# A written order for the first turns of a 64-unit pipeline, with two units begun beside the second Gram matrix

## The chip, the cores and the metric

The kernel runs on one core of one Trainium2 chip, as one launch, with all data in float32. The metric is device time in microseconds (us). The kernel before took 2868.09 us as the median of three runs (2866.86 to 2873.42).

## What is computed

The input is `x` of shape (16, 32, 128, 128). Two residual layers follow each other.

```
# layer 0
n = group_norm(x, 16 groups)
q, k, v = projections of n: 8 images are stacked into 256 channels, 8 heads of 64
x = x + Wout . (softmax(q k^T / 8) v) + bout        # attention over channels, not pixels
# layer 1
w = group_norm(x), in windows of 8x8 pixels;  y = layernorm(w) over the 32 channels
a = kan(y, groups of 16 along the window's height)  # kan(t): exp(-((layernorm(t) - g_i) / d)^2) for 8 g_i,
d = kan(y, groups of 16 along its width)            #   times a matrix, + silu(t) times a matrix, + bias
e = kan(y, the 32 channels)
out = x + w + kan(a + d + e, the 32 channels)
```

## The kernel before

**Layer 0 as a matrix.** Attention runs over channels, so all that it needs from the pixels is a 256 x 256 Gram matrix for each group `bp` of eight images. Two groups make two Gram matrices. `gram_load` brings 16 blocks of 2 MB (SP issues one half of a block, ACT the other), `gram_turn` transposes them on DVE (64 turns `m`, four to a block, into two alternating buffers, so turn m waits until turn m-2 has been summed), and `gram_sum` multiplies on PE (four strips of eight matmul records to a turn). `attention(bp)` then makes a matrix `pts[bp]` in 49 short steps that alternate between PE, DVE and ACT. Step 0 and 1 of `attention(1)` read the second Gram matrix out of its PSUM buffer and free it.

**Layer 1 as 64 units.** A unit is 128 partitions by 1024 values. Units 0 to 31 belong to the first eight images and need `pts[0]`; units 32 to 63 need `pts[1]`. For each unit, tasks run one after another:

- `load` (one transfer for two units), `layer0_norm` (PE steps 0, 2, 5; ACT steps 1, 3, 4, 6), `keep` (spills the unit to DRAM), `rows_norm` (PE step 0; DVE steps 1 to 3), `move` (eight transfers that exchange rows and partitions, `d<-yy`).
- `norm_a` and `norm_b` (PE steps 0, 4, 6; ACT steps 1, 2, 3, 5), `scale_a` and `scale_b` (DVE, two steps, line 1140), `seed_a` and `seed_b` (ACT, four steps of exponentials), `ladder_a` and `ladder_b` (DVE, seven products of basis functions, line 1169), `silus` (ACT).
- `products_a` and `products_b` (PE, accumulating in both PSUM buffers named X), `evict_a`, `move_back` (`ad_r<-ad`), `evict_z`; the sum of a unit goes through `norm_b` and `products_b` once more two turns later; then `again`, `result`, `store`.

In what follows, `norm_a.0.1` is step 0 of `norm_a` for unit 1, and `attention.21.1` is step 21 of `attention(1)`; the lists in the code count in the same way (name, step, unit or units behind).

**The order.** All engines execute their instructions in the order in which they are issued, and the kernel fixes that order itself. `Flow.run` holds all tasks as generators, keeps a planned time for each engine and each buffer, and repeatedly issues one step. `ORDER` gives, for PE, ACT, DVE and SP, the steps of one turn, with how many units behind each step is; `Flow.orders` repeats it for all turns. In `run`, the first step of an engine's list that isn't done and whose unit is below `first` is that engine's due step; steps that no list names (Gram matrices, attention, parameters) are fitted in where they are ready before the due step. `first` is `AHEAD` until the second Gram matrix is planned, and all units after that:

```
first = AHEAD if UNTIL not in self.found else units
```

With `AHEAD` 1, only unit 0 is taken up while the second Gram matrix is being summed.

**Buffers that matter here.** PSUM has two buffers X and two buffers Y. A Gram matrix holds one X; a unit's products take both X, so no product is issued before the second Gram matrix is finished and copied. `norm` takes both Y for its step 0 and for its step 6. There are six tiles `u`, three `R` and two `yy`; the Gram stage holds two `u`, two `R` and one `yy` until it ends, and the projections hold one `u` and `ad_r` on behalf of attention.

Of the kernel before, what the change touches and what calls it, by code (L numbers as in the profile page):

```python
# [72 lines left out]
    ),  # L73
}

FIRST = {"attention", "projections", "parameters"}
AHEAD, UNTIL = 1, ("gram", 1)
TURNS = 7


# [6 lines left out]
class Flow:  # L87
# [47 lines left out]

    def orders(self, units):

        out = {}
        for engine, text in ORDER.items():
            names = [(name, int(k), int(behind)) for name, k, behind in (t.split(".") for t in text.split())]  # L140
            out[engine] = [(name, m - behind, k) for m in range(units + TURNS) for name, k, behind in names]
        return out

    def run(self, tasks, units):
# [29 lines left out]
        for x in lines:  # L174
            on(x, None)
        heads = dict.fromkeys(orders, 0)
        while True:
            moved = True
# [45 lines left out]
            for c in able:  # L224
                name, engine = c[1]["at"][0], c[1]["asks"][0]
                at, unit = due.get(engine, (c[0] + 1, 0))
                late = c[0] > at or (c[0] == at and unit < AHEAD and name not in FIRST)
                if name in named or late or any(t + PATIENCE <= c[0] and kind in c[1]["asks"][2] for t, kind in kept):
# [1260 lines left out]
```

## Time and profile before

| | before |
|---|---|
| median of 3 runs (range) | 2868.09 us (2866.86 to 2873.42) |
| the profiled execution | 2870.64 us, span 2868.9 us |
| mean granted TensorE clock | 0.985 of full speed |
| busy PE, DVE, ACT (share of the span) | 2746.1 us (96%), 2685.3 us (94%), 2517.7 us (88%) |
| last matmul of the second Gram matrix ends | 221.8 us |
| first matmul of `products_a` | 244.7 us |
| `layer0_norm.0.n` starts, n = 0 to 6 | 145.6, 221.8, 237.8, 276.7, 330.6, 369.2, 409.0 us |

The busy shares are of the whole span; PE's records overlap, since sixteen small matmuls run side by side, so its busy time says that something was in flight, not that the array was full. From `layer0_norm.0.5` on, a turn takes about 39.6 us. Everything that the change touches lies ahead of that.

### The profile page before, as it was taken

Reading aid. Unit: us, or ns where it says so; the run is one execution under the profiler, and the core shown is the slowest. Engines: PE = TensorE matmul, PEld = TensorE weight load, DVE = VectorE, ACT = ScalarE, POOL = GpSimd, SP = SyncE. Lnnn points to the kernel's source line nnn. Section 1 sums busy time; section 2 is a strip of 40 time slices with the busy share of each in tenths; the row PEclk is TensorE's granted clock in tenths of the full one; section 3 lists DMA queues with packets and bytes.
Section 4 is the critical chain, followed back from the end, with each engine's and each line's share of the span. In section 5 each row is a group of like instructions: output and inputs, shape, how many; then the busy total and the mean of one; then the engine's idle time right before and its main releaser. Section 6 shows DMA issues by size and latency. Waiting matters only on the chain.

```text
span 2868.9 us, 100690 instructions
## 1 busy us (share of the span) xinstructions
PE 2746.1 (96%) x45955; PEld 1091.5 (38%) x45955; DVE 2685.3 (94%) x1793; ACT 2517.7 (88%) x2035; POOL 53.8 (2%) x109
## 2 busy tenths in 40 slices
PE   6999999999999999999999999999999999999985
PEld 6874433333333333333333333333333333333321
DVE  4747999999999999999999999999999999999986
ACT  0026899999999999999999999999999999999973
POOL 4200000000000000000000000000000000000000
PEclk9999999999999999999999999999999999999987
DMA  9652233333333333333333333333333333333311
GB/s 243 179 123 60 75 113 110 105 104 113 113 103 98 108 109 116 116 101 110 103 116 113 94 111 100 116 114 108 108 106 111 114 97 103 108 109 114 102 56 35
DMA packets 206152, 311.04 MB, mean 108 GB/s; under 512 B 24480, under 2 KB 156064, under 8 KB 205728
## 3 DMA queue, kind: packets, MB, share of 16 engines
q1 hardware_dynamic: 192512, 285.29, 33.8%
q10 hardware_dynamic: 9504, 16.85, 2.4%
q8 instruction: 362, 5.93, 0.9%
q0 software_dynamic: 3712, 2.46, 0.4%
q14 instruction: 62, 0.51, 0.1%
HBM read 103.18 MB, written 67.11 MB: 59 GB/s over the span
## 4 chain that ended last, share of the span: by engine, by line
PE 64%; DVE 20%; issue 6%; ACT 4%; DMA 4%; SPq 1%; DVEq 0%; ACTq 0%
PE X L436 25%; DVE u L1169 14%; PE X L1205 10%; PE Y L1004 7%; PE Y L436 4%; PE Y L1019 4%; PE X L1324 4%; PE X L684 3%; DVE yc L1140 3%; PE Y L1123 2%; PE Y L981 2%; DVE yy L1057 2%; DMA u<-in_x 1%; SPq L1241 1%; ACT u L1118 1%
## 5 line engine op out<-in xcount | busy, mean ns | idle before, releaser
L1169 DVE SCALAR_TENSOR_TENSOR u<-R,u 128x2048 f32<-128x2048 f32 x910 | 2043.4, 2286 | 38.0 <-ACT u L1154 17.0
L436 PE MATMUL X<-u,wt_a 32*32 32x512 f32 x16384 | 663.8, 605 | 11.2 <-ACT u L1154 4.1
L436 PE MATMUL X<-u,wt_b 32*32 32x512 f32 x16896 | 638.3, 605 | 16.3 <-ACT u L1154 9.4
L436 PEld LDWEIGHTS X<-u,wt_a 32*32 32x32 f32 x16384 | 302.7, 103 | 289.1 <-issue 136.4
L436 PEld LDWEIGHTS X<-u,wt_b 32*32 32x32 f32 x16896 | 224.7, 103 | 384.3 <-issue 194.2
L1140 DVE TENSOR_TENSOR yc<-yc,Y 128x1024 f32<-128x1024 f32 x260 | 305.4, 1216 | 10.6 <-PE Y L1123 7.5
L1149 ACT ACTIVATE u<-yc,vec 128x2048 f32<-128x2048 f32 x130 | 258.5, 1989 | 29.6 <-DVE yc L1140 24.7
L1115 ACT ACTIVATE yc<-Y 128x1024 f32<-128x1024 f32 x260 | 250.2, 1015 | 35.5 <-DMA u<-in_x 22.9
L1004 PE MATMUL Y<-x,pt 128*128 128x512 f32 x512 | 236.7, 605 | 31.5 <-DVE yc L1140 31.5
L1157 ACT ACTIVATE R<-yc,vec 128x2048 f32<-128x2048 f32 x130 | 259.5, 1996 | 2.5 <-DVE u L1169 1.5
L1151 ACT ACTIVATE R<-yc,vec 128x2048 f32<-128x2048 f32 x130 | 258.8, 1991 | 0.0
L1118 ACT ACTIVATE u<-yc 128x2048 f32<-128x2048 f32 x130 | 247.6, 1905 | 2.9 <-DVE u L1169 2.2
L1154 ACT ACTIVATE u<-u 128x2048 f32<-128x2048 f32 x130 | 247.1, 1901 | 0.0
L684 PE MATMUL X<-R 128*64 128x257 f32 (+3 forms) x2048 | 154.4, 312 | 22.8 <-DVE R L658 22.1
L983 ACT ACTIVATE lr<-Y,vec 128x512 f32<-128x512 f32 (+1 forms) x194 | 131.3, 677 | 45.0 <-PE Y L981 45.0
L1004 PEld LDWEIGHTS Y<-x,pt 128*128 128x128 f32 x512 | 92.2, 190 | 179.9 <-issue 92.9
L684 PEld LDWEIGHTS X<-R 128*64 128x64 f32 x2048 | 143.4, 142 | 42.3 <-DVE R L658 23.8
L981 PE MATMUL Y<-u,e 128*32 128x512 f32 x1040 | 139.6, 604 | 3.3 <-ACT u L1118 3.3
L1233 ACT ACTIVATE ad<-X,col 128x1024 f32<-128x1024 f32 x128 | 134.0, 1095 | 1.7 <-PE X L436 1.7
L1019 PE MATMUL Y<-xh,c 128*128 128x512 f32 x256 | 127.0, 618 | 2.4 <-ACT xh L1014 2.4
L984 ACT ACTIVATE lr<-lr 128x512 f32<-128x512 f32 (+1 forms) x194 | 122.4, 631 | 6.2
L1205 PE MATMUL X<-sd,silu_a 64*64 64x512 f32 x1024 | 124.7, 602 | 0.0
(210 smaller groups left out, 2472.9 us busy)
## 6 DMA issues: line engine op xcount, KB each, us to landing
xh<-xh SPq DMA_DIRECT2D x128, 512.0 KB
d<-yy SPq DMA_DIRECT2D x512, 128.0 KB
ad_r<-ad SPq DMA_DIRECT2D x512, 128.0 KB
x<-in_x SPq DMA_DIRECT2D x32, 1024.0 KB
out<-xh SPq DMA_DIRECT2D x256, 128.0 KB
u<-in_x SPq DMA_DIRECT2D x28, 256.0 KB
u<-in_x ACTq DMA_DIRECT2D x28, 256.0 KB
ad<-in_x SPq DMA_DIRECT2D x14, 256.0 KB
```

What stands on the lines that cost most here:

```text
L436: MM(dst(to, g_), lhsT=wt[32 * g_ : 32 * g_ + 32, :], rhs=rhs(g_, (to - turn[g_]) % 4), start=start, stop=stop,)
L684: MM(g[64 * q : 64 * q + 64, k, lo:hi], lhsT=t[:, b, at : at + 64], rhs=t[:, b, lo:hi], start=first, stop=last,)
L1004: MM(xp[:, u, :], lhsT=pts[bp][:, k, kk * P : (kk + 1) * P], rhs=xr[:, k, u * 512 : (u + 1) * 512], start=k == 0, stop=k == KK - 1,)
L1115: ACT(v[:, i * RB : (i + 1) * RB], flat(yt[i]), AF.Identity)
L1118: ACT(sq, v, AF.Square)
L1140: TT(v[:, o], v[:, o], flat(rb[i]), ALU.mult)
L1149: ACT(u, v, AF.Square, bias=bq)
L1151: ACT(up, v, AF.Exp, bias=bp_, scale=2.0)
L1154: ACT(u, u, AF.Exp, scale=-1.0)
L1157: ACT(down, v, AF.Exp, bias=bn, scale=-2.0)
L1169: STT(t, by, BIG, tiles[at[way]], ALU.min, ALU.mult)
L1205: MM(dst(i, f), lhsT=wt(i)[o, o], rhs=rhs(i, o), start=False, stop=False)
```

## The change

Three edits. A table `FIRST_TURNS` gives, for each of the four engines, a sequence of (step, unit) pairs for the units up to about 8. `Flow.orders` puts this sequence ahead of the repeated turns and drops from the turns what the sequence already has. `AHEAD` becomes 2, so units 0 and 1 are taken up while the second Gram matrix is being summed.

```
+FIRST_TURNS = {
+    "PE": (
+        "layer0_norm.0.0 layer0_norm.2.0 layer0_norm.5.0 rows_norm.0.0 layer0_norm.0.1 layer0_norm.0.2 "
+        "layer0_norm.2.1 norm_a.0.0 norm_b.0.0 layer0_norm.5.1 norm_a.4.0 rows_norm.0.1 norm_a.6.0 "
+        "layer0_norm.2.2 norm_b.4.0 norm_b.6.0 products_a.0.0 norm_a.0.1 products_a.1.0 products_a.2.0 "
...
+    "ACT": (
+        "layer0_norm.1.0 layer0_norm.3.0 layer0_norm.4.0 layer0_norm.6.0 layer0_norm.1.1 layer0_norm.1.2 "
...
+    "DVE": (
+        "rows_norm.1.0 rows_norm.2.0 rows_norm.3.0 rows_norm.1.1 rows_norm.2.1 scale_a.0.0 rows_norm.3.1 "
...
+    "SP": (
+        "load.0.0 load.0.2 keep.0.0 move.0.0 keep.0.1 move.0.1 move_back.0.0 move.0.2 move_back.0.2 move_back.0.3 "
...
+}
-AHEAD, UNTIL = 1, ("gram", 1)
+AHEAD, UNTIL = 2, ("gram", 1)
...
+        split = lambda text: [(name, int(a), int(b)) for name, a, b in (t.split(".") for t in text.split())]
         out = {}
         for engine, text in ORDER.items():
-            names = [(name, int(k), int(behind)) for name, k, behind in (t.split(".") for t in text.split())]
-            out[engine] = [(name, m - behind, k) for m in range(units + TURNS) for name, k, behind in names]
+            first = [(name, unit, k) for name, k, unit in split(FIRST_TURNS[engine])]
+            given = set(first)
+            turns = [(name, m - behind, k) for m in range(units + TURNS) for name, k, behind in split(text)]
+            out[engine] = first + [x for x in turns if x not in given]
         return out
```

No instruction is added, removed or resized: each engine issues the same ones in another order. What the two built programs issue around the second Gram matrix, "g12" standing for twelve strips of it (48 matmuls, 96 records) and "t8" for eight turns:

```
PE before:  rows_norm.0.0 g23 norm_a.0.0 g4 norm_b.0.0 g3 norm_a.4.0 g3 norm_a.6.0 g11 norm_b.4.0 g4 norm_b.6.0 g5 (end)
            layer0_norm.0.1 .2.1 .5.1 rows_norm.0.1 layer0_norm.0.2 attention.15.1 layer0_norm.2.2 products_a.0.0 ...
PE after:   rows_norm.0.0 layer0_norm.0.1 g3 layer0_norm.2.1 g9 norm_a.0.0 g4 norm_b.0.0 g3 layer0_norm.5.1 g11 norm_a.4.0
            rows_norm.0.1 g4 norm_a.6.0 g3 norm_b.4.0 g7 norm_b.6.0 g9 (end) layer0_norm.0.2 attention.2.1
            layer0_norm.2.2 attention.5.1 products_a.0.0 norm_a.0.1 products_a.1.0 ...
DVE before: t3 rows_norm.1.0 t1 rows_norm.2.0 t1 rows_norm.3.0 t7 scale_a.0.0 .1.0 t3 scale_b.0.0 .1.0 (end) attention.1.1
DVE after:  t3 rows_norm.1.0 .2.0 .3.0 t8 rows_norm.1.1 .2.1 scale_a.0.0 rows_norm.3.1 scale_a.1.0 t3
            scale_b.0.0 .1.0 ladder_a.0.0 t1 (end) attention.1.1
SP before:  block 14, move.0.0, block 15, keep.0.1, load.0.2, move.0.1
SP after:   block 14, move.0.0, keep.0.1, block 15, move.0.1, load.0.2
ACT before: block 14, block 15, norm_a.1.0 .2.0 .3.0 norm_b.1.0 ...
ACT after:  block 14, layer0_norm.1.1 .3.1 .4.1 norm_a.1.0 .2.0 .3.0 norm_b.1.0 silus.0.0 layer0_norm.6.1
            norm_b.2.0 block 15, norm_a.5.0 ...
```

Steps 21, 23 and 25 of `attention(1)` stood ahead of `layer0_norm.0.3` on PE and stand behind it now; `attention.25.1` is what frees `ad_r` for `move_back.0.0`. From `layer0_norm.0.4` to the turn of unit 8 the two programs issue the same steps in each turn with a few neighbours exchanged (for example `layer0_norm.0.5` behind one product more), and a few steps behind `layer0_norm.0.8` their orders become the same.

## The prediction

> **What bounds the kernel now.** I read the stretches of 50 us first, then PE's instructions in order of time around the end of the second Gram matrix, then who waited for whom. Columns of the first: the stretch, its length, busy us (records) of PE, weight loads, DVE, ACT, POOL, then granted clock, DMA share, GB/s.
>
> ```profile
> 150.00:200.00 50.00, 43.36 (x496) 36.49 (x498) 23.76 (x58) 6.16 (x9) 0.00 (x0) 0.86 0.67 157
> 200.00:250.00 50.00, 43.92 (x442) 27.51 (x451) 28.23 (x51) 35.15 (x36) 0.00 (x0) 0.97 0.21 66
> 250.00:300.00 50.00, 49.05 (x682) 20.88 (x661) 43.60 (x40) 36.79 (x31) 0.00 (x0) 0.97 0.26 74
> 300.00:350.00 50.00, 48.47 (x798) 19.59 (x798) 43.84 (x52) 41.32 (x35) 0.00 (x0) 0.93 0.20 56
> 350.00:400.00 50.00, 49.59 (x930) 18.56 (x911) 49.24 (x27) 48.47 (x40) 0.00 (x0) 1.00 0.32 97
> 450.00:500.00 50.00, 49.13 (x810) 17.23 (x812) 49.26 (x30) 49.03 (x40) 0.00 (x0) 1.00 0.39 118
> ```
>
> From 350 us on, PE, DVE and ACT are all about 98% busy: no engine can catch up, so a lead that the new order has when it enters the steady turns stays to the end, and so does a lag. Everything is decided between 177 us, where the orders part, and 331 us. There PE is the only engine that is nearly full (DVE idles 22 us in 200 to 250 alone).
>
> ```profile
> 177.44 13.00 PE L684 MATMUL X<-R 128*64 128x257 f32 x184
> 196.79 2.02 PE L436 MATMUL Y<-d,c 32*32 32x512 f32 x32 [6.34 <-DMA d<-yy]
> 218.92 2.96 PE L684 MATMUL X<-R 128*64 128x257 f32 x40
> 221.81 3.70 PE L1004 MATMUL Y<-x,pt 128*128 128x512 f32 x8
> ...
> 182.95 9.61 SPq L1098 DMA_DIRECT2D d<-yy  x8
> ...
> 185.63 2.21 ACTq L637 DMA_DIRECT2D u<-in_x  x4
> ```
>
> PE sums 23 strips in 13.00 us (0.57 each), then stands 6.34 us before `norm_a.0.0`, because `move.0.0` hasn't landed, with strips ready behind it. The last two lines say why it is late: it is issued from 182.95 on, in 9.61 us, and half a block (1 MB on ACT) joins it at 185.63. From 198.7 to the end at 221.8 PE doesn't wait. Then comes unit 1's beginning, and the first product only at 244.73.
>
> Two further losses matter: the clock (the same columns as above, in shorter stretches), and waits during the second attention.
>
> ```profile
> 302.40:305.80 3.40, 3.40 (x40) 1.72 (x40) 0.29 (x3) 1.69 (x1) 0.00 (x0) 0.50 0.00 0
> 305.80:309.30 3.50, 3.50 (x67) 1.55 (x68) 3.36 (x3) 0.00 (x0) 0.00 (x0) 0.54 0.00 0
> ```
>
> Who PE waited for from 222 to 410 us, in total, how often, the longest:
>
> ```profile
> PE Y L436 <- DMA d<-yy: 2.4, 1, 2.4
> PE Y L1019 <- ACT xh L1014: 2.4, 2, 1.2
> PE Y L1004 <- DVE yc L1140: 2.1, 4, 1.0
> ```
>
> **What the Trainium skill says.** "TensorE: Matmul & The Clock Gate", "What's actually happening": after an idle window of about 3.4 us the clock is halved until a busy one has passed. The trace agrees: 0.50 and 0.54 in two windows of that length behind the 16 one-column pairs of `attention.36.1`[...]; 3.3 us of full-speed work lost. The same page, "Step-by-step: what each phase is for": matmuls stay in program order, only weight loads are pulled ahead; the 6.34 us agree. "Trainium Kernel Development and Optimization", "Key Constraints": transfers from SP, ACT and POOL share 16 DMA engines; DMA share is 1.09 in 190.4 to 196.8, and `move.0.0` took 13.7 us from issue to use, `move.0.1` with less beside it 8.3 us (241.2 to 249.5).
>
> **The change, part by part.** Work is the same; only waits and cover differ. I walk PE's new order with the durations of before.
>
> *Unit 1 inside the Gram stage.* `layer0_norm.0.1` 3.6, `.2.1` 1.9, `.5.1` 1.0, `rows_norm.0.1` 1.1 (pitches of L1004, L1019, L981, L1052): 7.7 us of PE move ahead of the Gram matrix's end. ACT takes 4.7 us and DVE 2.6 us with them, both idle there. SP has `keep.0.1` (0.34) ahead of block 15 and `move.0.1` (5.9) ahead of `load.0.2`; `move.0.1` lands about 220, `load.0.2` starts at about 217 (227 before), each well ahead of its user at 228 or later: zero, unless the Gram stage's own transfers slip.
>
> *The wait for `move.0.0`.* Ahead of `norm_a.0.0` now stand 12 strips (6.8) and `layer0_norm.0.1`, `.2.1` (5.5): PE gets there at 190 as before. But `rows_norm.1.0` to `.3.0` run without turns between them (end 180.2 instead of 182.9), and ACT's half of block 15 is behind `norm_b.2.0`. At 180.2 about 0.9 MB of block 14 and 1.05 MB of the move are left; at 220 GB/s that is 8.9 us: landing at 189 to 191. I take 190.5; `norm_a.0.0` ends at 191.6, not 198.7. **6 us won**, and with it the slow clock behind the stall.
>
> *Two new waits.* From there: 41 strips (23.4) and seven steps (7.6) would end at 222.6. But DVE's order puts both `scale_a` steps and `rows_norm.3.1` ahead of turn 60 (they follow `norm_a.6.0`, done at 209.6; turn 60 ends at 214.2, PE wants it at 212.3: 1.9 us), and `scale_b.0.0`, `.1.0`, `ladder_a.0.0` (2.35 + 2.28) ahead of turn 63 (225.5 instead of 222.2: 3.4 us). SP's half of block 15 waits for turn 55, hence for `norm_a.0.0`, and lands near 200; ACT's is issued at 204.3 to 206.5 behind `silus.0.0` (5.5 with its table loads) and lands near 211, just under the 212.7 at which DVE wants it. Sum: **the Gram matrix ends at 227.9**, 6.1 later than 221.8, holding 7.7 us more work.
>
> *Behind it.* `layer0_norm.0.2` 3.6, a wait of 1.2 for `layer0_norm.1.2`, `.2.2` 2.0, `attention.5.1` 1.0: first product at 236 (244.7). `norm_a.0.1` finds its `d` in place (2.4 us gone), but waits 1.0 for a Y, since `ladder_a.1.0` is queued ahead of `attention.7.1` on DVE. Continuing so, `norm_a.6.1` is done at 263.1, against 275.3: a lead of 12.2. Attention steps 21, 23 and 25 (1.9 + 1.9 + 1.2) aren't done yet: **7.2 us of work ahead.**
>
> *The second attention takes some back.* Those steps now follow `layer0_norm.0.3`. `norm_b.6.1` needs both Y and waits for `attention.26.1` (1.6); `attention.29.1` for `scale_b` (1.1); `move_back.0.0` cannot start before `attention.25.1` frees `ad_r` at 276.6, issue 5.9 and landing 2.6 make 285 (0.4 to 1); `rows_norm.0.3` waits for `layer0_norm.6.3` behind an eviction (1.0); `norm_a.6.2` 0.4; `layer0_norm.0.4` 0.9. `layer0_norm.0.4` starts at 325.0 against 330.65, with 0.4 us of attention open: **5.2 ahead**. DVE, counted in the same way, is 6.1 ahead.
>
> *The clock.* Not in this walk: the halved windows behind `attention.36.1` (3.3 in before; here the products behind it meet partly waiting DVE, so some is free) and a window behind the 3.4 us wait at 222 to 225 (1.7). Bounds 0 and 5.0; I take 1.5, since DVE is ahead and covers part.
>
> *Turns of units 4 to 8.* Neighbours exchanged; before, PE waits about 0.5 us a turn at L1004 for `scale_a`, which one product more in front may cover. Zero; bounds 2 us either way.
>
> *Steady turns and tail.* Same order, 39.6 us a turn, both engines full; zero.
>
> **Sum:** 5.2 - 1.5 = 3.7, about 4 us less. Against the profiled execution (2870.6 = span 2868.9 + 1.7) that is 2866.6; that execution stood 2.5 above the median of the runs, so the forecast is 2868.1 - 4 = **2864 us**. About 0.2% (5.7 us) is what a measurement of this kernel can tell from no change, so 4 us counts as none.
>
> **Rivals.** *More gain.* The lead of 7.2 holds and the old waits go: after 275 us before lost 2.6 us of PE waits and 3.3 to the clock; if spreading attention avoids half of that, 10 us: 2858. For it: attention's small steps stand between products now. Against: DVE steps of attention sit behind 2.3 us ladders.
>
> *Slower: the move is still late.* All of the Gram stage now hangs on `move.0.0`: turn 55 and so block 15 on SP, `silus.0.0` and so block 15 on ACT wait behind `norm_a.0.0`. If it lands at 196.8 as before, everything behind is 6.3 later, the stall's slow clock (0.50, 1 us) comes back: 3.7 - 7.3 = -3.6; and if block 15, 6 us later too, then lands behind turn 60's place, 2 to 4 more: 7 us slower, 2875. It decides at a landing of 194.2: later than that, slower than before. For it: 13.7 us in before. Against: 1 MB less beside it.
>
> *No effect.* Lead and losses cancel: 2868.
>
> **How the numbers follow.** The sum's case 0.55 (gain 1 to 9; 0.17 of it above 5.7), more gain 0.22, slower 0.18 (0.17 of it beyond 0.2%), no effect 0.05. Faster 0.17 + 0.22 = 0.39; slower 0.17; within 0.2% the other 0.44. Likeliest case alone: 2859 to 2867. Range: down to 2853 (more gain with every bound in favour), up to 2876 (the late move with 1 us more).
>
> **What would show it.** Right: `norm_a.0.0` starts by 191 with no wait of several us; two waits of PE on DVE's turns near 213 and 223; Gram matrix done near 228; first product near 236; `layer0_norm.0.4` 3 to 6 us before 330.65, later ones keeping that lead at 39.6 a turn. Wrong: a wait for `d` at `norm_a.0.0`, or for block 15 near 213; a lead at `layer0_norm.0.4` that has gone by `layer0_norm.0.9`, which would mean that the exchanged neighbours, priced at zero, cost it.

## The result and the profile after

The changed kernel takes 2877.51 us (median of 16 runs, 2870.97 to 2885.31) against 2867.07 us (16 runs, 2862.84 to 2875.70) for the kernel before: a ratio of 1.0034, 95% interval 1.0025 to 1.0043, or about 10 us slower. The forecast was 4 us faster, and its range ended at 2876.

The profiled execution of after took 2872.32 us (span 2870.5), 5.2 us below the median of its runs, while that of before (2870.64) stood 3.6 above its own. The two traces are therefore read for where time goes, and the medians for how much.

The first turns went much as forecast. Stretches of the profile after; the columns are those of the prediction. The last line is of before, for the third.

```profile
150.00:200.00 50.00, 48.94 (x552) 37.58 (x550) 25.34 (x57) 19.27 (x19) 0.00 (x0) 0.94 0.62 148
200.00:250.00 50.00, 43.88 (x591) 25.63 (x587) 35.42 (x43) 30.98 (x32) 0.00 (x0) 1.00 0.25 65
500.00:550.00 50.00, 41.82 (x706) 14.96 (x705) 40.95 (x24) 39.99 (x32) 0.00 (x0) 0.93 0.26 75
550.00:600.00 50.00, 49.59 (x947) 19.56 (x943) 49.22 (x27) 49.01 (x40) 0.00 (x0) 1.00 0.35 106
...
500.00:550.00 50.00, 49.57 (x865) 18.71 (x866) 49.51 (x28) 48.51 (x39) 0.00 (x0) 1.00 0.39 118
```

From 150 to 200 us PE is busy 48.9 us instead of 43.4. The surprise is the third line: between 500 and 550 us PE, DVE and ACT are each busy 8 to 9 us less than before, in the midst of turns that are otherwise full. The lead shows the same. `layer0_norm.0.n` starts, after minus before:

| n | 0 | 4 | 6 | 8 | 9 | 10 | later |
|---|---|---|---|---|---|---|---|
| us | -2.9 | -7.1 | -6.5 | -5.1 | -4.9 | +2.9 | +2.2 to +5.1 |

The -2.9 at n = 0 comes before the orders part (in the kept traces this start lies between 3.5 us ahead of before's and 2.3 behind it). Counted from there, after leads by 4.2 us at unit 4, 3.6 at unit 6 and 2.1 at unit 9 in this execution. Then one turn of 48.5 us instead of 39.6 turns the lead into a lag, which stays.

### The profile page after: what moved, and what is told of

It reads as the page before. It is cut to its first block, busy times and chain, and to the rows that moved or that the text cites. A ratio compares the mean times of both kernels' runs of the same rounds, so it can differ in the third digit from the quotient of the medians.

```text
span 2870.5 us, 100677 instructions
## 1 busy us (share of the span) xinstructions
PE 2740.8 (95%) x45955; PEld 1085.8 (38%) x45955; DVE 2685.9 (94%) x1793; ACT 2518.7 (88%) x2035; POOL 53.7 (2%) x109
## 4 chain that ended last, share of the span: by engine, by line
PE 64%; DVE 20%; issue 6%; ACT 5%; DMA 3%; SPq 1%; DVEq 0%; ACTq 0%
PE X L530 25%; DVE u L1263 14%; PE X L1299 10%; PE Y L1098 7%; PE Y L530 4%; PE Y L1113 4%; PE X L1418 4%; PE X L778 3%; DVE yc L1234 3%; PE Y L1217 2%; PE Y L1075 2%; DVE yy L1151 2%; SPq L1335 1%; ACT u L1243 1%; ACT ad L1327 1%
## 5 line engine op out<-in xcount | busy, mean ns | idle before, releaser
L1263 DVE SCALAR_TENSOR_TENSOR u<-R,u 128x2048 f32<-128x2048 f32 x910 | 2043.6, 2286 | 39.2 <-ACT u L1248 17.2
L1098 PE MATMUL Y<-x,pt 128*128 128x512 f32 x512 | 236.7, 605 | 30.4 <-DVE yc L1234 30.4
L778 PE MATMUL X<-R 128*64 128x129 f32 (+3 forms) x2048 | 153.3, 309 | 27.5 <-DVE R L752 26.5
L1077 ACT ACTIVATE lr<-Y,vec 128x512 f32<-128x512 f32 (+1 forms) x194 | 131.3, 677 | 40.3 <-PE Y L1075 40.3
L1098 PEld LDWEIGHTS Y<-x,pt 128*128 128x128 f32 x512 | 92.1, 189 | 178.4 <-issue 92.6
L1327 ACT ACTIVATE ad<-X,col 128x1024 f32<-128x1024 f32 x128 | 134.1, 1095 | 1.1 <-PE X L530 1.1
```

What stands on the lines that cost most here:

```text
L778: MM(g[64 * q : 64 * q + 64, k, lo:hi], lhsT=t[:, b, at : at + 64], rhs=t[:, b, lo:hi], start=first, stop=last,)
L1098: MM(xp[:, u, :], lhsT=pts[bp][:, k, kk * P : (kk + 1) * P], rhs=xr[:, k, u * 512 : (u + 1) * 512], start=k == 0, stop=k == KK - 1,)
L1263: STT(t, by, BIG, tiles[at[way]], ALU.min, ALU.mult)
```

## What happens in that turn

SP's instructions from 490 to 530 us, in order of time: start, duration, queue, line, what goes where, how many. L1335 is `move_back`, L1454 `store`, L1135 `keep`, L1464 `again`, L1192 `move`. First the kernel before, where `store` is L1360, `move_back` L1241, `keep` L1041, `again` L1370 and `move` L1098:

```profile
495.44 5.10 SPq L1098 DMA_DIRECT2D d<-yy  x8
500.64 1.12 SPq L1041 DMA_DIRECT2D xh<-xh  x1
505.52 2.99 SPq L1360 DMA_DIRECT2D out<-xh  x4
522.00 6.02 SPq L1241 DMA_DIRECT2D ad_r<-ad  x8
528.12 0.53 SPq L1370 DMA_DIRECT2D xh<-xh  x1
```

The same view of after:

```profile
490.03 3.19 SPq L1192 DMA_DIRECT2D d<-yy  x5
493.32 0.54 SPq L1135 DMA_DIRECT2D xh<-xh  x1
516.90 5.84 SPq L1335 DMA_DIRECT2D ad_r<-ad  x8
522.83 3.02 SPq L1454 DMA_DIRECT2D out<-xh  x4
525.95 0.42 SPq L1464 DMA_DIRECT2D xh<-xh  x1
```

Before has `store.0.3` ahead of `move_back.0.6` in SP's order; after has them exchanged: the table says `move_back.0.6 store.0.3`. SP issues in order. The result that the store writes out is ready at 500.6, when this DVE instruction ends:

```profile
499.27 1.28 DVE L1445 SCALAR_TENSOR_TENSOR xh<-xh,l0c,X 128x1024 f32<-128x1024 f32 x1
```

But at 493.9 SP came to `move_back.0.6`, whose `ad` isn't evicted before 516.9. So the store stands behind a transfer that waits 23.5 us. It is issued 22 us after its result was ready, and 17 us later than before issued it, which was at once (505.5). SP's waits from 470 to 530 us, as engine and line, whom it waited for, then us in total, how often, the longest (the row names L1077, which ACT starts as the eviction, L1327, ends):

```profile
SPq L1335 <- ACT lr L1077: 23.5, 1, 23.5
```

A wait of that length on SP is harmless in itself: before, SP stands 13.5 us ahead of the same transfer (508.5 to 522.0). What counts is who is behind it. The store reads a tile `xh`, there are two of them, and the next writer of that tile is `layer0_norm.1.9` on ACT (L1108). ACT's instructions of after; the last bracket is idle time before, and what ended it:

```profile
526.34 1.99 ACT L1243 ACTIVATE u<-yc,vec 128x2048 f32<-128x2048 f32 x1
535.99 1.20 ACT L1108 ACTIVATE xh<-Y,l0c 128x1024 f32<-128x1024 f32 x1 [7.67 <-DMA out<-xh]
```

ACT stands 7.67 us until the store has landed, and with it everything that ACT has in its order behind this step. PE waits at `norm_b.6` for a row statistic, and DVE for PE:

```profile
PE Y L1217 <- ACT lr L1078: 7.6, 1, 7.6
DVE yc L1234 <- PE Y L1217: 8.7, 1, 8.7
```

Since all three are full in these turns, nothing makes it up.

The store's own landing is part of it. Stretches of after, same columns as above:

```profile
526.00:533.00 7.00, 4.89 (x58) 0.82 (x56) 6.01 (x4) 2.33 (x2) 0.00 (x0) 1.00 0.31 115
533.00:536.00 3.00, 0.00 (x0) 0.00 (x0) 0.00 (x0) 0.01 (x1) 0.00 (x0) 0.80 0.12 46
```

In the last 3 us no engine does anything, and the DMA engines are 12% busy at 46 GB/s. 512 KB leave so slowly that the store lands 10 us after the end of its issue (525.85 to about 535.9).

## The experiments

Each number is a median; in brackets behind a ratio its 95% interval against runs of before on the same chip, whose medians were 2867 to 2870 us.

**One pair in SP's table, in after.**

```
-"... move.0.6 move_back.0.6 store.0.3 again.0.4 ..."
+"... move.0.6 store.0.3 move_back.0.6 again.0.4 ..."
```

> The changed kernel with two neighbours exchanged in the table's SP row: store.0.3 ahead of move_back.0.6. Theory A (one transfer in the wrong place on SP): in the changed kernel store.0.3 stands behind move_back.0.6, which waits 23.5 us for its eviction, so the tile xh that unit 9 needs is freed late, and ACT, and all engines behind it, stand 7.7 us at layer0_norm.1.9. With the exchange that wait is gone, the lead of 4.9 us that the changed kernel had at layer0_norm.0.9 stays: about 5 us faster than before, 2862. Rival B (the wait is one symptom; later turns or the second attention lose the time): the wait goes but the time stays above before, 2869 to 2873, since the changed kernel's median is 10 us above before and the wait that the trace shows is only 7.7.

Measured: 2866.35 us (13 runs), 0.9995 (0.9986 to 1.0004): 11.2 us less than after, and level with before. The cause that theory A names is confirmed; its 5 us faster than before did not come (at most 4.0 by the interval). Its SP order in time, two lines of it:

```profile
502.80 3.00 SPq L1454 DMA_DIRECT2D out<-xh  x4
519.12 5.93 SPq L1335 DMA_DIRECT2D ad_r<-ad  x8
```

The store has been issued by 505.8, and ACT has no wait on `xh` for a DMA between 400 and 600 us. One pair of entries in SP's list accounts for the whole loss against before.

**The same pair exchanged in before, and nothing else.**

```
+if engine == "SP":
+    i, j = (out[engine].index((name, unit, 0)) for name, unit in (("store", 3), ("move_back", 6)))
+    out[engine][i], out[engine][j] = out[engine][j], out[engine][i]
```

> The kernel before, with one exchange in its repeated SP order: store.0.3 behind move_back.0.6, nothing else. Theory A: store.0.3 is issued at about 528 instead of 505.5, takes 3 us to issue and about 10 to land, so layer0_norm.1.9, due at 532, waits until about 541: 8 to 10 us slower than before, 2876. Rival B: before is 5 us later at that place than the changed kernel and has slack there; within 2 us of before.

Measured: 2877.95 us (9 runs), 1.0032 (1.0022 to 1.0042): 9.2 us slower than before (0.0032 of 2868), with none of the table's order. SP in this kernel:

```profile
523.22 6.04 SPq L1244 DMA_DIRECT2D ad_r<-ad  x8
529.36 3.02 SPq L1363 DMA_DIRECT2D out<-xh  x4
```

and ACT:

```profile
542.86 1.20 ACT L1017 ACTIVATE xh<-Y,l0c 128x1024 f32<-128x1024 f32 x1 [8.21 <-DMA d<-yy]
```

The same 8 us before the same instruction. The bracket names another transfer; L1017 reads no `d`, but writes the `xh` that the store still reads. (In the run that follows, the third late store shows the same wait, 7.8 us, with `out<-xh` as its end.)

**Three such pairs in before**, at units 3, 20 and 40:

```
+    for u in (3, 20, 40):
+        i, j = (out[engine].index((name, unit, 0)) for name, unit in (("store", u), ("move_back", u + 3)))
+        out[engine][i], out[engine][j] = out[engine][j], out[engine][i]
```

> The kernel before with three such exchanges: store.0.3 behind move_back.0.6, store.0.20 behind move_back.0.23, store.0.40 behind move_back.0.43. Theory A (each late store holds up all engines once, and steady turns have no slack to make it good): three times 9.7 us, 2897. Rival F (only the first one matters, since its turn has a transfer of the next pair of units beside it, or the engines catch up between them): 2878 to 2886.

Measured: 2896.96 us (5 runs), 1.0096 (1.0082 to 1.0110): 27.5 us, 9.2 us for each. The trace has three turns of 49.3, 49.0 and 50.0 us. The turns are those of units 9, 26 and 46, against 39.5 to 40.6 without a late store. The price is the same wherever the pair stands, so it has nothing to do with the first turns.

**Two units beside the Gram matrix, without the table** (before with `AHEAD` 2):

```
-AHEAD, UNTIL = 1, ("gram", 1)
+AHEAD, UNTIL = 2, ("gram", 1)
```

> The kernel before with AHEAD 2 and no table. Theory A (the lead comes from unit 1's beginning beside the Gram matrix, the wait from the table's SP row): SP keeps store.0.3 ahead of move_back.0.6, no wait at unit 9; without the table DVE puts the last turns ahead of scale_b and ladder_a.0.0, but attention steps stand ahead of the first ladders; a lead of 3 to 7 us at layer0_norm.0.6, total 2861 to 2865. Rival C (the written sequence makes the lead): within 2 us of before, 2867.

Measured: 2867.82 us (13 runs), 0.9995 (0.9987 to 1.0003). No difference, as rival C said: the second unit alone brings no lead (0.4 us at unit 6 in its trace).

**A table only up to `layer0_norm.0.6`**, then the repeated turns of before. Its lists are written anew from the order in which after issues its steps: by the traces PE, ACT and DVE issue the same as in after up to about 396 us, but neither the neighbours exchanged later nor the late store are there. The edit against before, with the last line of PE's list:

```
+FIRST_TURNS = {
+    "PE": (
...
+        "norm_a.6.4 products_b.3.3 layer0_norm.0.6 "
...
-AHEAD, UNTIL = 1, ("gram", 1)
+AHEAD, UNTIL = 2, ("gram", 1)
...
```

> The changed kernel's order written out up to the turn of layer0_norm.0.6 on PE, ACT and DVE and up to move_back.0.2 on SP, and the repeated order of before from there on. Theory A: no wait at unit 9, and the 1.4 us that the changed kernel loses between layer0_norm.0.6 and .8, where neighbours are exchanged, are kept: lead 6.4 us, 2860.5. Rival D (the exchanged neighbours cost nothing lasting): as with store.0.3 alone put right, 2862.

Measured: 2865.56 us (21 runs), 0.9988 (0.9981 to 0.9995), or 3.4 us faster than before (1.4 to 5.4). That is what the forecast gave to the whole change, and less than either theory expected of this run (2860.5 and 2862).

**The same shortened table with `AHEAD` 1.**

```
-AHEAD, UNTIL = 2, ("gram", 1)
+AHEAD, UNTIL = 1, ("gram", 1)
```

> The order of e4_regular_turns with AHEAD 1: unit 1 begins behind the second Gram matrix again, and attention's steps follow where the planner then fits them. Theory G (two units beside the Gram matrix and the written sequence make the lead together; two units alone gave none, 0.9995): no lead, 2866 to 2872. Rival H (the written sequence is enough): 2864 to 2866, as e4.

Measured: 2890.97 us (5 runs), 1.0074 (1.0061 to 1.0086): 21 us slower, outside what was expected. The lag is there from `layer0_norm.0.2` (+22.5 us) and is 17 to 22 us from `layer0_norm.0.4` to the end. With one unit taken up, unit 0's `norm_b` ends and attention's steps come behind the Gram matrix and ahead of the first product; PE's largest waits on that stretch are 5.3 and 2.7 us in attention steps. So neither the table nor the second unit is worth anything alone; the lead is that of both together. How the 21 us divide was not taken further.

**The turns first.** The prediction put 5.3 us of PE's waits down to two DVE turns that stand behind steps of unit 0 and 1. Starting from the shortened table, whose trace has the same two waits as after (1.62 and 3.26 us), four DVE steps are held until those turns are planned:

```
+HOLD = {("rows_norm", 3, 1): 60, ("scale_a", 1, 0): 60, ("scale_b", 0, 0): 63, ("ladder_a", 0, 0): 63}
...
+if (name, k, unit) in HOLD and ("turned", HOLD[name, k, unit]) not in self.found:
+    continue
```

> As e4_regular_turns, but DVE takes turn 60 ahead of rows_norm.3.1 and scale_a.1.0, and turn 63 ahead of scale_b.0.0, scale_b.1.0 and ladder_a.0.0. Theory A (the two waits of PE for DVE's turns, 1.6 and 3.3 us in the changed kernel, and the halved clock that may follow the second, are real losses of the written order): the Gram matrix ends 3 to 5 us earlier, and 3 us of it stay: 0.9978 of before, 2862. Rival E (the lead is set behind the Gram matrix, by seeds and ladders that take as long as before): the Gram matrix ends earlier and the first ladders start no earlier; within 1 us of e4, 2865.5.

Measured: 2863.14 us (11 runs), 0.9971 (0.9960 to 0.9983): 8.3 us faster than before. PE around the end of the Gram matrix, in after:

```profile
187.82 1.15 PE L530 MATMUL Y<-d,c 32*32 32x512 f32 x32 [0.77 <-issue]
...
211.24 4.06 PE L778 MATMUL X<-R 128*64 128x257 f32 x56 [1.62 <-DVE R L752]
215.23 1.14 PE L1217 MATMUL Y<-lr,back_b 32*128 32x512 f32 x8
216.30 2.96 PE L778 MATMUL X<-R 128*64 128x257 f32 x40
222.53 2.41 PE L778 MATMUL X<-R 128*64 128x257 f32 x32 [3.26 <-DVE R L752]
224.87 3.70 PE L1098 MATMUL Y<-x,pt 128*128 128x512 f32 x8
...
232.75 1.14 PE L530 MATMUL X<-u,wt_a 32*32 32x512 f32 x32
```

and in this kernel, where the Gram matrix is L756 and `layer0_norm.0.2` L1076:

```profile
212.28 4.61 PE L756 MATMUL X<-R 128*64 128x257 f32 x64 [1.04 <-DVE R L730]
216.82 1.14 PE L1195 MATMUL Y<-lr,back_b 32*128 32x512 f32 x8
217.89 2.41 PE L756 MATMUL X<-R 128*64 128x257 f32 x32
221.34 3.67 PE L1076 MATMUL Y<-x,pt 128*128 128x512 f32 x8 [1.04 <-DMA x<-in_x]
...
229.19 1.14 PE L508 MATMUL X<-u,wt_a 32*32 32x512 f32 x32
```

Of the waits of 1.62 and 3.26 us one of 1.04 is left, and the first product starts at 229.2 instead of 232.8. A new wait of 1.04 us has come up: the load of unit 2 is late by that much. Against the shortened table this is 4.9 us less (0.0017, about 1 to 9), where the waits on DVE are 3.8 us shorter. So both waits that the prediction's walk found were real, and rival E, that the lead is set behind the Gram matrix, doesn't fit; how much of each wait came through to the end isn't measured more closely than that.

**Store in eighths.** The landing of 10 us was the next question. The Trainium skill, "DMA: Bandwidth & Descriptors", "Why a DMA increments its semaphore by 16 and not by 1", says that a transfer is spread over the largest number of engines up to 16 that divides the slowest dimension of both its sides. The store is cut into four transfers whose DRAM side begins with a dimension of 2, which would be two engines; cut into eight of 16 partitions it begins with 16:

```
-                for b in range(4):
+                for b in range(8):
                     nc.sync.dma_start(
-                        out=out_rows[bp * KK + kk, b, :, :, j * RB : (j + 1) * RB], in_=xh[32 * b : 32 * b + 32, :]
+                        out=out_rows[bp * KK + kk, b // 2, b % 2, :, j * RB : (j + 1) * RB],
+                        in_=xh[16 * b : 16 * b + 16, :],
                     )
```

In after:

> The changed kernel, with store writing a unit in eight transfers of 16 partitions instead of four of 32; order as it is. In the changed kernel the four transfers end their issue at 525.9 and the tile is free at 535.9, while the queues move about 50 GB/s with a tenth of the engines busy. Theory K (each transfer of 32 partitions has 2 as its slowest count on the DRAM side and is served by two engines, so half a megabyte takes 10 us; with 16 as the slowest count it is served by 16): issue 5 us, landing 2 to 3, tile free at 530 to 531 against a need at 528.3; the wait at layer0_norm.1.9 shrinks from 7.7 to 2 to 3, total 2868 to 2871. Rival L (the landing is slow because it is a write to DRAM): wait 8 to 10 as before or more, 2878 to 2881.

In the kernel before with the late store:

> e2_before_late_store with the same store: store.0.3 is as late, but lands sooner. Theory K: of the 9.7 us, 2 to 4 are left, 2870 to 2872. Rival L: 2878 to 2880.

In the kernel with the turns first:

> e5_turns_first with the same store. No wait on a store is left in e5, so both theories say no change: 0.9971 of before, 2862; up to 1 us slower if the four more issues on SP delay a transfer behind them.

And in before alone, to separate the two effects:

> The kernel before with store in eight transfers of 16 partitions, nothing else. Before ends 14.0 us after its last result on DVE, the kernels with the store in eighths about 7. Theory M (what e8, e9 and e10 have beyond the removed wait is the last store's landing): 6 to 7 us faster than before, 0.9976, 2861.5; the wait-free turns unchanged. Rival N (it is elsewhere in the turns): span behind the last result shorter, total less than 3 us faster.

| | store in four | store in eight |
|---|---|---|
| before | 1 | 0.9977 (0.9970 to 0.9985), 2863.38 us, 21 runs |
| before, late store | 1.0032 (1.0022 to 1.0042) | 0.9982 (0.9974 to 0.9989), 2864.38 us, 22 runs |
| after | 1.0034 (1.0025 to 1.0043) | 0.9972 (0.9962 to 0.9983), 2860.77 us, 13 runs |
| turns first | 0.9971 (0.9960 to 0.9983) | 0.9956 (0.9940 to 0.9972), 2856.36 us, 6 runs |

Down the first column a late store costs 9 us; down the second 1.4 us, which its interval doesn't tell from nothing. In after with eighths, SP's order is that of after, and the store is issued as late:

```profile
517.91 5.87 SPq L1335 DMA_DIRECT2D ad_r<-ad  x8
523.87 3.77 SPq L1454 DMA_DIRECT2D out<-xh  x8
527.74 0.37 SPq L1465 DMA_DIRECT2D xh<-xh  x1
```

but ACT waits only 0.2 us at `xh`. While the store is being issued, with the end of `move_back` still under way, the DMA share is 0.78, where after has 0.38 from 523 to 526 us:

```profile
523.80:527.70 3.90, 3.71 (x12) 1.51 (x16) 3.90 (x4) 3.88 (x4) 0.00 (x0) 1.00 0.78 169
```

A part was missed by the expectations of the first three, which put these kernels 6 to 10 us too slow. They counted the turn, and left out that the last store of the program is on the path too. Behind the last result nothing computes. Before, from there to the span's end:

```profile
2854.90:2868.90 14.00, 0.00 (x0) 0.00 (x0) 0.00 (x0) 0.00 (x0) 0.00 (x0) 0.50 0.10 37
```

and the same stretch of before with the store in eighths:

```profile
2855.20:2861.60 6.40, 0.00 (x0) 0.00 (x0) 0.00 (x0) 0.00 (x0) 0.00 (x0) 0.50 0.47 82
```

37 GB/s over 14.0 us is one store of 512 KB (0.52 MB), at a tenth of the DMA engines; in eighths the tail is 7.6 us shorter, and this kernel as a whole gains 6.6 us (2869.71 times 0.0023; the interval is 4.3 to 8.6). The tail is 14.0 us in all nine kept traces with the store in four, and 6.4 in all four with eight. Two engines of the 27 GiB/s that the same page states under "Specifications" would carry 58 GB/s at best (an estimate); the 37 to 46 GB/s here and the share of 0.10 to 0.12 (two of sixteen is 0.125) agree with that. The packets of the two tails, store in four first, say it more directly:

```profile
DMA packets 136, 0.52 MB, mean 37 GB/s; under 512 B 8, under 2 KB 8, under 8 KB 136
DMA packets 256, 0.52 MB, mean 82 GB/s; under 512 B 128, under 2 KB 128, under 8 KB 256
```

The data goes in 128 packets of 4 KB in both. Beside them stand small packets of 4 bytes, two for each of the four transfers and sixteen for each of the eight. By the packets' start and duration two are under way at a time for 10.6 of 11.1 us in the first, and 11 to 15 for 3.5 of 4.0 us in the second. So it isn't smaller pieces that win: a packet of 4 KB takes longer in the second, 365 ns against 176 on average, but many more run side by side.

With turns first and the store in eighths, 2856.36 us, the kernel beats both of the pair: 12.6 us below before (8.0 to 17.2).

## Why the prediction was wrong

**The step that failed** is "Turns of units 4 to 8", priced at "zero; bounds 2 us either way". It looked at PE alone: the wait at L1004 for `scale_a`, and products exchanged. Its bound held for PE, if barely: from unit 4 to unit 8 the lead falls by 1.2 to 2.0 us in the three traces of after's order. SP's queue was not walked in those turns. There, one exchange put a store, ready at 500.6 us, behind a transfer whose source isn't due before 516.9, and that is 11.2 us by the medians, 7.7 us of ACT's wait in the profile. The sum without it:

| | forecast | measured |
|---|---|---|
| lead at `layer0_norm.0.6`, counted from `layer0_norm.0.0` | 3.7 us | after's order 1.4, 3.6, 5.1 (three traces); table up to unit 6: 3.6 |
| lead lost to exchanged neighbours on PE, units 6 to 9 | 0 | 0.7 to 1.5 us (the same three traces) |
| after without the late store, whole kernel against before | 3.7 us faster | 1.4 us faster (4.0 faster to 1.1 slower) |
| loss by the exchanged neighbours on SP | not counted | 11.2 us |

The prediction had a sign for this: a lead that has gone by `layer0_norm.0.9` would mean that the exchanged neighbours cost it. The lead was gone one unit later, and the neighbours were those of SP. The rival "the move is still late" named 2875 us, close to the 2877.5 measured, but what it describes did not occur; that the number is near is chance.

**The walk to the end of the Gram matrix held.** `norm_a.0.0` started at 187.8 with a wait of 0.8 us (forecast 190.5; this execution was 2.9 us early). The two waits for turns were 1.62 and 3.26 us (1.9 and 3.4), the Gram matrix ended at 224.9 (227.9), the first product started at 232.8 (236), and `layer0_norm.0.4` at 323.6 (325.0). One sum of the prediction doesn't close from what it shows: 7.2 us of work ahead, less the waits listed behind it (5.4 to 6.0), plus the 2.6 that before lost there by the prediction's own count, leaves 3.8 to 4.4 and not 5.2. The trace has 4.2 at that place, counted from `layer0_norm.0.0`.

**A lead stays to the end.** That was said of the steady turns, and the kernels without a late store fit it:

| | lead at unit 6, us | whole kernel, us |
|---|---|---|
| two units only | 0.4 | -1.4 (-3.7 to +0.9) |
| after, store first | 1.4 | -1.4 (-4.0 to +1.1) |
| table up to unit 6 | 3.6 | -3.4 (-5.4 to -1.4) |
| turns first | 8.7 | -8.3 (-11.5 to -4.9) |

The first column is of one execution each, and its close agreement with the second is in part luck. Four kernels beside before itself have its order up to unit 6, and their leads there are -3.3, 0.0, 2.8 and 3.2 us; after's order has 1.4, 3.6 and 5.1. One trace thus tells such a lead only to about 3 us. The profiled execution of turns first was the fastest of its runs, 8.4 us under their median; the same order with the store in eighths has a lead of 6.6. What stands by the medians is that the table up to unit 6 is faster than before and turns first faster still. A lag stays too: the 9 us that the late store in before has cost by unit 10 are 8.5 at unit 63.

**The clock** was put at 1.5 us with bounds of 0 and 5. Behind `attention.36.1` after has one halved stretch of 3.4 us (1.6 us lost) where before had two:

```profile
303.00:306.40 3.40, 3.40 (x43) 0.82 (x18) 0.01 (x1) 1.91 (x1) 0.00 (x0) 0.54 0.00 0
306.40:309.80 3.40, 3.40 (x90) 1.51 (x105) 1.74 (x5) 0.14 (x1) 0.00 (x0) 1.00 0.02 5
```

The prediction says that the trace of before agrees there with an idle window as the cause. It does so less plainly than that: in the stretch ahead of the halved ones PE's records leave no idle time, with the short one-column matmuls in it:

```profile
299.00:302.40 3.40, 3.40 (x26) 2.90 (x24) 2.21 (x2) 3.40 (x4) 0.00 (x0) 0.97 0.23 86
```

Behind the wait of 3.26 us, which the prediction priced at 1.7 us, the clock stayed at 1.00 in after, and fell in the kernel with only the store's place restored, as this stretch of that kernel shows:

```profile
222.00:225.40 3.40, 3.40 (x26) 3.11 (x28) 0.00 (x0) 0.00 (x0) 0.00 (x0) 0.52 0.00 0
```

That is 1.6 us, but drawn anew in each execution: the two programs have the same order up to there. It could make most of the 2.2 us by which that kernel's lead at unit 6 is the smaller.

**What stays open.** The late store costs 11.2 us by the medians of after, and 9.2 in the other two kernels. With the intervals of the ratios (about 7.5 to 14.8, and 6.3 to 12.0 for one late store in before) these don't differ. The profiled waits of ACT are 7.7 to 8.2 us and the turns 48.5 to 50.0 us long instead of 39.6 to 40.6; whether more than one turn is lost in after isn't settled. The lead that after's order brings without the late store is 1.4 us by the medians, and can't be told from nothing.

**How it could have been seen.** The diff shows `move_back.0.6 store.0.3` in SP's part of the table. Two rows of the profile before are enough to price it: in SP's timeline the store at 505.52 and `move_back` at 522.00. An exchange delays the store to behind 522 + 6 us, hence by 22.5 us. The tile has two buffers, and in each turn of 39.6 us `layer0_norm.1` and `again` fill one each. The last store of before lands 14.0 us behind its result, so this one would land near 542, and ACT wants the buffer at 533.3 in the profile before:

```profile
533.34 1.19 ACT L1014 ACTIVATE xh<-Y,l0c 128x1024 f32<-128x1024 f32 x1
```

That is 8.7 us, an estimate from the profile before alone, where 9.2 was measured.

## What to carry to other kernels

When an order is rewritten, walk every queue that it is written for, those that only issue transfers included: for each exchange ask when each of the two could go at the earliest, because the ready one inherits the wait of the other. A transfer that is behind another's wait costs nothing by itself; it costs when somebody needs the buffer that it frees, so count the buffers and find the next writer. And where a lead is won ahead of steady turns in which all engines are full, one lost turn later takes it back whole.

## What the runs showed of the hardware

- A store of 512 KB in four transfers whose DRAM side begins with a dimension of 2 lands 10 us after the end of its issue, or 14.0 us after the last result at the end of the program; in eight transfers of 16 partitions that tail is 6.4 us. Two packets of 4 KB run side by side in the first and 11 to 15 in the second. This was worth 6.6 us of the whole kernel.
- Behind a wait of about 3.3 us on PE the clock was halved for 3.4 us in one execution, and not in another of the same order (0.52 and 1.00). It was also halved (0.50 and 0.54) behind a stretch in which PE's records leave no idle time.
- The trace can name a transfer that wasn't needed as what ended an idle time: in the kernel with one late store ACT's wait for `xh` is put down to `d<-yy`, which that instruction doesn't read.
